# First queries repeated by PE with 0/1 matrices, keys projected ahead of queries, identity turns at the start, and scatters of rows moved, in a relative-attention and mixture-of-experts kernel

## The chip, the cores and the metric

The kernel runs on one core of one Trainium2 chip. The metric is device time in microseconds (us), the median of several executions; lower is better. The engines are PE (matmuls; its weight loads are shown apart as PEld), DVE, ACT and POOL, and SP, which here issues transfers. ACT and POOL issue some transfers too.

## The reference

`x` has 16 batches of 512 tokens with 128 features. The first half is attention with 16 heads of 8 features and relative positions, the second a mixture of 16 experts with one chosen for each token, and each has a layernorm (LN) ahead of it and one behind it.

```python
q, k, v = proj(Wq, bq), proj(Wk, bk), proj(Wv, bv)          # x normalized first
idx = jnp.clip(r[None, :] - r[:, None], -M, M) + M           # M = 128
rpk, rpv = rel_k[idx], rel_v[idx]
scores = (einsum('bhqd,bhkd->bhqk', q, k) + einsum('bhqd,qkd->bhqk', q, rpk)) / sqrt(hd)
w = softmax(scores)
out = einsum('bhqk,bhkd->bhqd', w, v) + einsum('bhqk,qkd->bhqd', w, rpv)
x = x + layernorm(out @ Wo.T + bo)
x = x + layernorm(moe(layernorm(x)))                         # top 1 of 16 experts, and a shared one
```

## The kernel before

All is in fp32. The attention loop (line 787) has 16 iterations for a batch, 256 in all, and a short tail. Iteration i belongs to batch b = i // 16, to c = (i % 16) // 4 and n = i % 4; k is i % 16. An iteration takes 32 queries (rows n * 128 + c * 32 on) of all 16 heads, as four tiles of 128 rows (32 queries times four heads) and 512 keys.

One iteration makes, in this order: the scores of its own queries (`scores`, line 377): four matmuls of the keys `km` with the expanded queries `qb`, and 32 small ones of the relative keys `relk` with the expanded queries `qr`; the turns (transposes by PE, `turn`, line 420) of the weights of iteration i - 1; DVE's negated maximum `nmax` and ACT's exponential for its own four tiles; the attention of iteration i - 5 (`attend`, line 473): 32 matmuls `pa<-wT,v`, and 48 short ones `pa<-wT,relv` for the near relative values (`attend_near`, line 509); and one more job for the single bank of `ps_o`, called `spare`. Score tiles have five banks of PSUM (`ps_s`), turns two (`ps_t`).

`qb` repeats the queries of 16 groups of eight with a 0/1 mask of heads, `qr` repeats them over positions with the mask `mq`. For `qr` the queries stand in another order on the partitions (`qz`): ACT writes `qp` (line 268), SP copies it to DRAM (`qd`, line 273), and 16 small transfers bring it back as `qz` (`queries_turned`, line 280). `expand` (line 357) then makes `qb` and `qr` on POOL, for the four iterations of one c, three iterations ahead (line 876).

The batch's own work is spread over the loop: statistics of the next x (k = 0 and 2), LN's root on POOL (`rstd_of`, line 75, a power), normalization, the turn of x (k = 6), queries (7), keys (14), values (15). `keys_mixed` and `keys_advance` keep, on POOL, the four copies of the keys `km` with the end values of the relative keys added.

For batch 0 the same work stands ahead of the loop (lines 768 to 785): statistics, LN with DVE, turn of x, queries, keys, `qz` (half of the transfers on ACT's queue), values, `expand(0, 0)`, `keys_mixed`, the load of x of batch 1 and `later_loads` (line 172).

`route` (line 602) takes a batch's attention output through both LNs, the router's logits and the counting of rows per expert, in 16 steps; it is a generator, and the loop takes one step at each of the listed places (line 865). Its last four steps are `pool.indirect_dma_start` (line 761): POOL scatters 128 rows of `pay` to `rows` in DRAM. Route r starts in k = 6 of batch r + 1; its scatters stand at the ends of k = 6, 7, 9 and 10 of batch r + 2, behind that iteration's key advance on POOL's queue. In k = 0, 4, 8 and 12 stands `sums` (line 428): DVE's reciprocal `rt` and POOL's copy `rb`, which PE turns, ACT copies to `R`, and POOL multiplies to `Rh` and `Rz`.

The order on PE, ACT, DVE, POOL and SP in the attention part is the order of the program text (`InOrder`, line 39); engines wait for each other by semaphores. After the loop, 73 blocks of 128 rows go through their experts (from line 881); between iterations 10 and 30 SP clears `rows` in 20 pieces (line 809).

```python
        for f in (x_turn, queries, keys):
            f(0)()
        queries_turned(0)
        values(0)()
        expand(0, 0)
```

Of the kernel before, what the change touches and what calls it, by code (L numbers as in the profile page):

```python
# [17 lines left out]
P = 128  # L18
# [3 lines left out]
HD = 8  # L22
# [28 lines left out]
def relative_attention_then_moe(  # L51
# [42 lines left out]
    with ExitStack() as actx:  # L94
# [11 lines left out]
        def load_x(b):  # L106
            x_sb[b] = bp.tile([P, NKT, D], F32, tag="x", name=f"x_sb{b}", bufs=4)

            for n in range(NKT):
                sp_q.dma_start(  # L110
                    x_sb[b][n * 32 : (n + 1) * 32], x[b, n * P : (n + 1) * P].rearrange("(c q) d -> q c d", q=32)
                )

        load_x(0)


        wq = wp.tile([P, D], F32, name="wq")
        wk = wp.tile([P, D], F32, name="wk")
# [14 lines left out]
        LR = 511  # L133
        rext = wp.tile([HD, LR], F32, name="rext")
        act.dma_start(bq_c, bq.rearrange("(p o) -> p o", o=1))
        act.dma_start(wq, WqT)
        act.dma_start(rext[:, 127 : 127 + NR], rel_kT)
        act.dma_start(wk, WkT)
        act.dma_start(bk_c, bk.rearrange("(p o) -> p o", o=1))
        act.dma_start(wv, WvT)  # L140
        act.dma_start(bv_r.rearrange("p h d -> p (h d)"), bv.partition_broadcast(P))
# [2 lines left out]
        for i in range(2):  # L144
            sp_q.dma_start(
                kend[:, i : i + 1], bass.AP(rel_kT.tensor, rel_kT.offset + i * (NR - 1), [[0, H], [NR, HD], [1, 1]])
            )
        act.mul(bq_c, bq_c, qscale)
        bk_hi = wp.tile([P, 1], F32, name="bk_hi")
        relk = wp.tile([P, 504], F32, name="relk")  # L150
# [69 lines left out]
        def bank(shape, name):  # L220
            return ps_o.tile(shape, F32, tag="o", name=name)
# [6 lines left out]
        def x_norm(b, eng=pool, between=None):  # L228

            mv = batch[b]["mv"]  # L230
            rs = rstd_of(sp, mv, NC, "lx", dve, pool)
            if between is not None:
                between()
            xn = bp.tile([P, NC, D], F32, tag="xn", name=f"xn{b}", bufs=1)
            for c in range(NC):
                eng.tensor_scalar(
                    xn[:, c, :], x_sb[b][:, c, :], mv[:, c, 0:1], rs[:, c : c + 1],
                    ALU.subtract, ALU.mult,
                )
            batch[b]["xn"] = xn  # L240
# [13 lines left out]
        def queries(b):  # L254


            xT = batch[b]["xT"]
            pq = bank([P, S], f"pq{b}")
            pe.matmul(
                pq.rearrange("p (c n q) -> p c n q", n=NKT, c=NC), wq,  # L260
                xT.rearrange("p (n c q) -> p c n q", n=NKT, c=NC), start=True, stop=True,
            )
            qp = bp.tile([P, TQ, S // TQ], F32, tag="qp", name=f"qp{b}")
            qz = bp.tile([P, 8, S // TQ], F32, tag="qz", name=f"qz{b}")
            batch[b].update(qp=qp, qz=qz)

            def leave():
                act.activation(
                    qp.rearrange("p q t -> p t q"), pq.rearrange("p (t q) -> p t q", q=TQ),
                    AF.Identity, bias=bq_c, scale=qscale,  # L270
                )
                qd = dp.tile([P, TQ, S // TQ], F32, tag="qd", name=f"qd{b}", bufs=2)
                sp_q.dma_start(qd, qp)
                batch[b]["qd"] = qd
                if b > 0:
                    queries_turned(b)

            return leave

        def queries_turned(b):  # L280
            qz, qd = batch[b]["qz"], batch[b]["qd"]
            for e in range(2):
                for i in range(TQ):
                    r = e * 64 + (7 - i) * HD
                    queue = act if b == 0 and i % 2 else sp_q
                    queue.dma_start(
                        qz[r : r + HD], qd[e * 64 : (e + 1) * 64, i, :].rearrange("(h d) t -> d h t", d=HD)
                    )

        def keys(b):  # L290

            pk = bank([P, S], f"pk{b}")
            pe.matmul(pk, wk, batch[b]["xT"], start=True, stop=True)
            kT = bp.tile([P, S], F32, tag="kT", name=f"kT{b}")
            batch[b]["kT"] = kT
            batch[b]["km"] = {}

            def leave():
                if b == 0:

                    km, hi = mixed(b, 0)
                    act.activation(km[:, 0:hi], pk[:, 0:hi], AF.Identity, bias=bk_c)
                    act.activation(km[:, hi:S], pk[:, hi:S], AF.Identity, bias=bk_hi)
                act.activation(kT, pk, AF.Identity, bias=bk_c)

            return leave

# [29 lines left out]
        def values(b):  # L337

            xT = batch[b]["xT"]
            pv = bank([P, NKT, D], f"pv{b}")  # L340
            for t in range(NKT):
                pe.matmul(pv[:, t, :], xT[:, t * P : (t + 1) * P], wv, start=True, stop=True)
            v = bp.tile([P, 3, NKT, D], F32, tag="v", name=f"v{b}")
            batch[b]["v"] = v

            def leave():
                if b == 0:
                    for t, n in ((v_lo, 0), (v_hi, 1)):
                        dve.tensor_copy(t, vend[:, n : n + 1, :].to_broadcast([P, H, HD]))
                row = lambda t, n: t.rearrange("p h d -> p (h d)").unsqueeze(1).to_broadcast([P, n, D])  # L350
                dve.tensor_add(v[:, 0], pv, row(bv_r, NKT))
                pool.tensor_add(v[:, 1, 0:2], v[:, 0, 0:2], row(v_lo, 2))
                pool.tensor_add(v[:, 2, 2:4], v[:, 0, 2:4], row(v_hi, 2))

            return leave

        def expand(b, c):

            bt = batch[b]
            tt = slice(c * 16, (c + 1) * 16)  # L360
            qb = up.tile([P, 16, HH, TQ], F32, tag="qb", name=f"qb{b}_{c}")
            pool.tensor_mul(
                qb,
                bt["qp"][:, :, tt].rearrange("p q t -> p t q").unsqueeze(2).to_broadcast([P, 16, HH, TQ]),
                mh4.unsqueeze(1).unsqueeze(3).to_broadcast([P, 16, HH, TQ]),
            )
            qr = up.tile([P, 16, 8, TQ], F32, tag="qr", name=f"qr{b}_{c}")
            pool.tensor_mul(
                qr,
                bt["qz"][:, :, tt].rearrange("p h t -> p t h").unsqueeze(3).to_broadcast([P, 16, 8, TQ]),  # L370
                mq.unsqueeze(1).unsqueeze(1).to_broadcast([P, 16, 8, TQ]),
            )
            batch[b, c] = (qb, qr)

        ORDER = (0, 2, 1, 3)

# [51 lines left out]
        def sums(b, c):  # L428

            rt = sp.tile([P, NKT, HG], F32, tag="rt", name=f"rt{b}_{c}")  # L430
            dve.reciprocal(rt, wts[b, c][1])
            rb = up.tile([P, NKT, HG, 32], F32, tag="rb", name=f"rb{b}_{c}", bufs=1)
            pool.tensor_copy(rb, rt.unsqueeze(3).to_broadcast([P, NKT, HG, 32]))
            batch[b, c, "rb"] = rb
# [333 lines left out]
        for c in range(NC):  # L768
            x_stats(0, c)
        x_norm(0, dve, relative_keys)  # L770
        dve.tensor_reduce(mh4, mh.rearrange("p (g h) -> p h g", h=HH), AX.X, ALU.add)
        dve.tensor_add(mq, mi[:, 0, :], mi[:, 1, :])
        dve.tensor_reduce(mz, mz4.rearrange("p g q -> p q g"), AX.X, ALU.add)
        dve.tensor_reduce(msum, mj.rearrange("p j g d -> p g d j"), AX.X, ALU.add)
        dve.tensor_add(bk_hi, bk_c, kend[:, 1:2])
        for f in (x_turn, queries, keys):
            f(0)()
        queries_turned(0)
        values(0)()
        expand(0, 0)  # L780
        for n in range(1, NKT):
            keys_mixed(0, n)
        if B > 1:
            load_x(1)
        later_loads()
        routes = {}
        for i in range(total + 24):
# [15 lines left out]
                routes[b - 1, 1] = route(b - 1, NC - 1, NC)  # L803
            if n == 0 and 0 <= i - 4 < total:
                sums(*at(i - 4)[:2])
                spare = lambda: sums_turn(*at(i - 4)[:2])
            if n == 1 and i >= 9 and i - 9 < total:
                spare = lambda: output(*at(i - 9)[:2])
            if 10 <= i < 30:
                clear_rows((i - 10) * NBLK // 20, (i - 9) * NBLK // 20)  # L810
            if nxt is not None:
# [48 lines left out]
            for r in sorted(routes):  # L860

                if r[0] < B - 2:
                    turns = i - (r[0] + 1) * 16 - 6 in (0, 1, 2, 3, 4, 5, 6, 7, 12, 13, 14, 15, 16, 17, 19, 20, 21)
                else:
                    turns = {7: 2, 9: 0, 12: 0, 13: 2, 15: 2}.get(k, 1) if live else 1
                for _ in range(turns):
                    bank_user = next(routes[r], StopIteration)
                    if bank_user is StopIteration:  # L870
                        del routes[r]
                        break
                    elif bank_user is not None:
                        bank_user()()
# [198 lines left out]
```

## Time and profile before

| what | value |
|---|---|
| median of 3 timed runs | 1917.79 us (1917.73 to 1917.93) |
| profiled execution, its own time | 1931.33 us |
| its span, first to last instruction | 1929.6 us |
| mean granted TensorE clock | 0.988 |
| busy share: PE, PEld, DVE, ACT, POOL | 97%, 72%, 79%, 63%, 51% |
| start of the first `nmax` (iteration 0) | 26.39 us |
| start of the last iteration's `nmax` | 1652.34 us |
| length of batches 2 to 14, `nmax` to `nmax` | 101.9 to 102.5 us |

The profile is of one execution with the recording on, which is why its time lies above the median. A row of a timeline has the start, the time, the engine, the line, the operation, the tiles written and read, the number of merged instructions, and in brackets the idle time of the engine just before with what ended it. Line 47 is the helper that keeps the order, so most rows carry L47 and are told apart by their tiles; buffer numbers are left out of names. "issue" means that the engine waited for nothing that the profile shows. The starts of the four `nmax` of an iteration give each iteration's length; in batches 2 to 14 iterations of the same k agree within some hundredths of a microsecond.

### The profile page before, as it was taken

How to read it: one execution, taken by the hardware profiler on the slowest of the kernel's cores; microseconds unless marked ns; L12 is line 12 of the kernel's file. 1: busy time of each engine (PE TensorE's matmuls, PEld its weight loads, DVE VectorE, ACT ScalarE, POOL GpSimd, SP SyncE). 2: the span in 40 equal slices, each digit the busy share in tenths (PEclk: the TensorE clock that was granted, in tenths of full speed). 3: DMA queues.
4: the chain of work that ended last, by engine and by line, in shares of the span. 5: the costliest groups of instructions: out<-in, count | busy, mean ns of one | idle time of the engine just before them, and what ended most of it. 6: DMA issues, size and time to landing. Idle time of an engine off the chain costs nothing. (4 is left out here: it accounts for less than half of the span.)

```text
span 1929.6 us, 88255 instructions
## 1 busy us (share of the span) xinstructions
PE 1863.7 (97%) x38268; PEld 1383.0 (72%) x38268; DVE 1528.7 (79%) x4009; ACT 1207.7 (63%) x3077; POOL 989.8 (51%) x1389
## 2 busy tenths in 40 slices
PE   6999999999999999999999999999999999779997
PEld 3667776776777777676767676776767776579997
DVE  4777787878788878788888888787878787757776
ACT  3666666666666666666666666666666665257775
POOL 4345455546455554546454555454645545236666
PEclk9999999999999999999999999999999999879999
DMA  2321100000000000000000000000000000066662
GB/s 77 65 35 40 17 23 5 15 14 5 24 5 24 4 24 3 25 3 25 3 24 5 24 4 16 12 13 16 5 18 5 18 3 9 9 176 180 183 182 87
DMA packets 88328, 68.64 MB, mean 36 GB/s; under 512 B 26440, under 2 KB 74341, under 8 KB 87809
## 3 DMA queue, kind: packets, MB, share of 16 engines
q1 hardware_dynamic: 81248, 53.60, 10.3%
q0 software_dynamic: 4384, 8.57, 1.4%
q8 instruction: 301, 4.93, 1.0%
q10 hardware_dynamic: 2304, 0.80, 0.2%
q14 instruction: 91, 0.74, 0.1%
HBM read 44.79 MB, written 18.75 MB: 33 GB/s over the span
## 5 line engine op out<-in xcount | busy, mean ns | idle before, releaser
L47 ACT ACTIVATE w<-ps,nmax 128x512 f32<-128x512 f32 x1024 | 699.0, 693 | 554.4 <-DVE nmax L47 554.0
L47 DVE TENSOR_REDUCE nmax<-ps 128x1 f32<-128x512 f32 x1024 | 655.1, 681 | 226.4 <-PE ps L47 225.2
L47 PE MATMUL pt<-ident,w 128*128 128x128 f32 x4096 | 562.0, 280 | 4.4 <-DVE wT L47 3.8
L47 PEld LDWEIGHTS pt<-ident,w 128*128 128x128 f32 x4096 | 439.7, 141 | 125.6 <-issue 85.7
L47 DVE COPY wT<-pt 128x512 f32<-128x512 f32 x512 | 348.3, 680 | 1.1 <-PE pt L47 0.7
L47 ACT COPY wT<-pt 128x512 f32<-128x512 f32 x512 | 300.9, 588 | 28.5 <-PE pt L47 26.5
L47 PE MATMUL ps<-km,qb 32*128 32x512 f32 x2048 | 298.4, 647 | 3.5 <-POOL qb L47 3.5
L47 PEld LDWEIGHTS ps<-relk,qr 64*32 64x32 f32 x8192 | 124.4, 106 | 227.6 <-issue 183.9
L47 PE MATMUL pa<-wT,v 128*32 128x128 f32 x8192 | 276.7, 276 | 2.5 <-DVE oz L47 1.4
L47 PE MATMUL ps<-relk,qr 64*32 64x288 f32 (+4 forms) x8192 | 275.5, 378 | 0.0
L47 PEld LDWEIGHTS pa<-wT,v 128*32 128x32 f32 x8192 | 208.1, 109 | 45.2 <-issue 36.0
L47 ACT ACTIVATION_READ_ACCUMULATOR w<-ps,nmax 128x1 f32 x1024 | 211.8, 207 | 0.0
L47 PE MATMUL pa<-wT,relv 128*32 128x48 f32 (+1 forms) x12288 | 199.3, 211 | 6.2 <-issue 5.4
L47 POOL TENSOR_TENSOR Rh<-R,mh 128x512 f32<-128x512 f32 x64 | 66.6, 1040 | 261.0 <-ACT R L47 253.8
L47 PEld LDWEIGHTS pa<-wT,relv 128*32 128x32 f32 x12288 | 186.8, 110 | 11.1 <-issue 11.1
L47 POOL TENSOR_TENSOR qr<-qz,mq 128x1024 f32<-128x1024 f32 x64 | 137.3, 2146 | 0.0
L47 PEld LDWEIGHTS ps<-km,qb 32*128 32x128 f32 x2048 | 82.4, 184 | 59.9 <-issue 32.0
L47 POOL TENSOR_SCALAR km<-kT,kend 128x32 f32<-128x32 f32 (+2 forms) x223 | 115.6, 520 | 1.7 <-PE ps L47 0.9
L47 POOL COPY km<-kT 128x32 f32<-128x32 f32 (+3 forms) x207 | 53.0, 261 | 113.8 <-ACT kT L47 113.8
L47 POOL DMA_INDIRECT out_dram<-f,to x73 | 75.9, 1039 | 46.8 <-issue 26.9
L47 DVE TENSOR_TENSOR od<-pa,Rh 128x128 f32<-128x128 f32 x256 | 72.9, 285 | 32.6 <-PE pa L47 29.7
L47 POOL COPY rb<-rt 128x512 f32<-128x512 f32 x64 | 39.2, 612 | 112.3 <-DVE rt L47 112.1
(168 smaller groups left out, 2331.0 us busy)
## 6 DMA issues: line engine op xcount, KB each, us to landing
gu<-_L_ffn_gate_up_proj_dram SPq DMA_DIRECT2D x73, 256.0 KB
dn<-in_L_ffn_down_proj_dram SPq DMA_DIRECT2D x73, 128.0 KB
rows<-zero SPq DMA_DIRECT2D x19, 266.0 KB
xc<-rows SPq DMA_DIRECT2D x8, 532.0 KB
x_sb<-in_L_attn_x_dram SPq DMA_DIRECT2D x64, 64.0 KB
qd<-qp SPq DMA_DIRECT2D x16, 256.0 KB
qz<-qd SPq DMA_DIRECT2D x248, 16.0 KB
relv<-vext SPq DMA_DIRECT2D x1, 1536.0 KB
```

What stands on the lines that cost most here:

```text
L47: return lambda *a, **k: self.tc.keep_in_program_order(op(*a, **k))
```

## The change

Five things are changed, all in the attention part.

1. `warm(52)`: PE makes 52 turns of the identity into a tile that nobody reads, as its first work.
2. Loads: `wk` goes ahead of `wq` on ACT's queue; x of batch 1 is loaded on SP right behind `kend`, ahead of `kext`, and not after the preparation of batch 0.
3. The preparation of batch 0: keys are projected ahead of queries, into a bank of `ps_s`. ACT writes the first `km`, then only the first 16 of 64 columns of `qp`, then `kT`, then the other 48. PE repeats the first 16 columns with eight 0/1 matrices `sel` (128x128 each), which POOL makes behind LN's root by one memset and eight selects, in a buffer of tag `wT`; DVE makes the first `qb`, and the first `qr` from PE's banks. Only the other 48 columns go through DRAM to `qz`, with all 16 transfers on SP.
4. The values of batch 0 become the `spare` job of iteration 2.
5. Routes 0 to 12 take their last four steps, the scatters, in the iterations with n = 0, right behind `sums` (so behind `rb` and ahead of `Rh` on POOL): k = 8 and 12 of batch r + 2, and k = 0 and 4 of batch r + 3. Routes 13 to 15 stay as they were.

```diff
+        def warm(n):
+            idle = ps_t.tile([P, NKT, P], F32, tag="t", name="idle")
+            for t in range(n):
+                pe.transpose(idle[:, t % NKT, :], ident, ident)
+        warm(52)
...
+        act.dma_start(wk, WkT)
         act.dma_start(wq, WqT)
         act.dma_start(rext[:, 127 : 127 + NR], rel_kT)
-        act.dma_start(wk, WkT)
...
+        if B > 1:
+            load_x(1)
         act.mul(bq_c, bq_c, qscale)
...
+        def repeat_queries(rep_q):
+            for h in range(8):
+                pe.matmul(
+                    rep_q[h // 4][:, h % 4].rearrange("p t q -> p q t"), sel[:, h * P : (h + 1) * P],
+                    batch[0]["qp"][:, :, 0:16], start=True, stop=True,
+                )
+        def expand_first(rep_q):
...
+            dve.tensor_mul(
+                qb,
+                batch[0]["qp"][:, :, 0:16].rearrange("p q t -> p t q").unsqueeze(2).to_broadcast([P, 16, HH, TQ]),
+                mh4.unsqueeze(1).unsqueeze(3).to_broadcast([P, 16, HH, TQ]),
             )
+            for i in range(2):
+                dve.tensor_mul(
+                    qr[:, :, i * 4 : (i + 1) * 4, :].rearrange("p t h q -> p h t q"), rep_q[i],
+                    mq.unsqueeze(1).unsqueeze(1).to_broadcast([P, 4, 16, TQ]),
+                )
...
+        sel = up.tile([P, 8 * P], F32, tag="wT", name="sel")
+        nc.gpsimd.memset(sel, 0.0)
+        for h in range(8):
+            nc.gpsimd.affine_select(
...
-        for f in (x_turn, queries, keys):
-            f(0)()
-        queries_turned(0)
-        values(0)()
-        expand(0, 0)
+        x_turn(0)()
+        leave_k = keys(0)
+        leave_q = queries(0)
+        rep_q = [ps_t.tile([P, 4, 16, TQ], F32, tag="t", name=f"rep_q{i}") for i in range(2)]
+        leave_k()
+        leave_q(0, 16)
+        repeat_queries(rep_q)
+        leave_k(False)
+        expand_first(rep_q)
+        leave_q(16, S // TQ)()
         for n in range(1, NKT):
             keys_mixed(0, n)
-        if B > 1:
-            load_x(1)
         later_loads()
...
                 sums(*at(i - 4)[:2])
+                for r in sorted(routes):
+                    if r[0] < B - 3 and i - (r[0] + 1) * 16 - 6 >= 18:
+                        if next(routes[r], StopIteration) is StopIteration:
+                            del routes[r]
...
+            if i == 2:
+                spare = lambda: values(0)
...
-                if r[0] < B - 2:
+                if r[0] < B - 3:
+                    turns = i - (r[0] + 1) * 16 - 6 in (0, 1, 2, 3, 4, 5, 6, 7, 12, 13, 14, 15)
+                elif r[0] < B - 2:
                     turns = i - (r[0] + 1) * 16 - 6 in (0, 1, 2, 3, 4, 5, 6, 7, 12, 13, 14, 15, 16, 17, 19, 20, 21)
```

More of the change, by code (lines that the diff above doesn't have):

```diff
@@ L265, in queries, with leave, turned @@
             batch[b].update(qp=qp, qz=qz)
-            def leave():
+            qd = dp.tile([P, TQ, S // TQ], F32, tag="qd", name=f"qd{b}", bufs=2)
+            def leave(t0=0, t1=S // TQ):
                 act.activation(
-                    qp.rearrange("p q t -> p t q"), pq.rearrange("p (t q) -> p t q", q=TQ),
+                    qp[:, :, t0:t1].rearrange("p q t -> p t q"),
+                    pq[:, t0 * TQ : t1 * TQ].rearrange("p (t q) -> p t q", q=TQ),
                     AF.Identity, bias=bq_c, scale=qscale,
                 )
-                qd = dp.tile([P, TQ, S // TQ], F32, tag="qd", name=f"qd{b}", bufs=2)
-                sp_q.dma_start(qd, qp)
-                batch[b]["qd"] = qd
+                if b == 0 and t0 == 0:
+                    return
+                sp_q.dma_start(qd[:, :, t0:t1], qp[:, :, t0:t1])
+                def turned():
+                    for e in range(2):
+                        for i in range(TQ):
+                            r = e * 64 + (7 - i) * HD
+                            sp_q.dma_start(
+                                qz[r : r + HD, :, t0:t1],
+                                qd[e * 64 : (e + 1) * 64, i, t0:t1].rearrange("(h d) t -> d h t", d=HD),
+                            )
                 if b > 0:
-                    queries_turned(b)
-            return leave
[L280 to L288, printed above, removed]
+                    turned()
+                return turned
+            return leave
         def keys(b):
-            pk = bank([P, S], f"pk{b}")
+            pk = bank([P, S], f"pk{b}") if b > 0 else ps_s.tile([P, S], F32, tag="s", name="pk0")
             pe.matmul(pk, wk, batch[b]["xT"], start=True, stop=True)
@@ L296, in keys, with leave @@
             batch[b]["km"] = {}
-            def leave():
-                if b == 0:
+            def leave(first=b == 0):
+                if first:
                     km, hi = mixed(b, 0)
@@ L303, in leave @@
                     act.activation(km[:, hi:S], pk[:, hi:S], AF.Identity, bias=bk_hi)
-                act.activation(kT, pk, AF.Identity, bias=bk_c)
+                else:
+                    act.activation(kT, pk, AF.Identity, bias=bk_c)
             return leave
@@ L355, in values, with expand @@
             return leave
-        def expand(b, c):
+        def expand(b, c, eng=pool, parts=((0, 16),)):
             bt = batch[b]
-            tt = slice(c * 16, (c + 1) * 16)
             qb = up.tile([P, 16, HH, TQ], F32, tag="qb", name=f"qb{b}_{c}")
-            pool.tensor_mul(
+            qr = up.tile([P, 16, 8, TQ], F32, tag="qr", name=f"qr{b}_{c}")
+            batch[b, c] = (qb, qr)
+            for t0, t1 in parts:
+                n, tt = t1 - t0, slice(c * 16 + t0, c * 16 + t1)
+                eng.tensor_mul(
+                    qb[:, t0:t1],
+                    bt["qp"][:, :, tt].rearrange("p q t -> p t q").unsqueeze(2).to_broadcast([P, n, HH, TQ]),
+                    mh4.unsqueeze(1).unsqueeze(3).to_broadcast([P, n, HH, TQ]),
+                )
+                eng.tensor_mul(
+                    qr[:, t0:t1],
+                    bt["qz"][:, :, tt].rearrange("p h t -> p t h").unsqueeze(3).to_broadcast([P, n, 8, TQ]),
+                    mq.unsqueeze(1).unsqueeze(1).to_broadcast([P, n, 8, TQ]),
+                )
@@ new lines, in repeat_queries @@
+        def repeat_queries(rep_q):
[3 more added lines that the diff above has]
+                    batch[0]["qp"][:, :, 0:16], start=True, stop=True,
+                )
+        def expand_first(rep_q):
+            qb = up.tile([P, 16, HH, TQ], F32, tag="qb", name="qb0_0")
+            qr = up.tile([P, 16, 8, TQ], F32, tag="qr", name="qr0_0")
+            batch[0, 0] = (qb, qr)
+            dve.tensor_mul(
@@ L363, in expand @@
                 qb,
-                bt["qp"][:, :, tt].rearrange("p q t -> p t q").unsqueeze(2).to_broadcast([P, 16, HH, TQ]),
+                batch[0]["qp"][:, :, 0:16].rearrange("p q t -> p t q").unsqueeze(2).to_broadcast([P, 16, HH, TQ]),
                 mh4.unsqueeze(1).unsqueeze(3).to_broadcast([P, 16, HH, TQ]),
             )
[L367 to L372, printed above, removed]
@@ L373, in expand @@
-            batch[b, c] = (qb, qr)
+            for i in range(2):
+                dve.tensor_mul(
+                    qr[:, :, i * 4 : (i + 1) * 4, :].rearrange("p t h q -> p h t q"), rep_q[i],
+                    mq.unsqueeze(1).unsqueeze(1).to_broadcast([P, 4, 16, TQ]),
+                )
         ORDER = (0, 2, 1, 3)
@@ L770, in relative_attention_then_moe @@
         x_norm(0, dve, relative_keys)
+        sel = up.tile([P, 8 * P], F32, tag="wT", name="sel")
+        nc.gpsimd.memset(sel, 0.0)
+        for h in range(8):
+            nc.gpsimd.affine_select(
+                sel[:, h * P : (h + 1) * P].rearrange("p (e j d) -> p e j d", e=2, j=TQ),
+                sel[:, h * P : (h + 1) * P].rearrange("p (e j d) -> p e j d", e=2, j=TQ),
+                [[-64, 2], [0, TQ], [-1, HD]], ALU.not_equal, 1.0, base=-h * HD, channel_multiplier=1,
+            )
         dve.tensor_reduce(mh4, mh.rearrange("p (g h) -> p h g", h=HH), AX.X, ALU.add)
```

## The prediction

> **What bounds the kernel now.** I read the page's slices first, then the timeline of the first 50 us, then the start of every iteration: a block of 32 queries takes four iterations, a batch 16 (k = 0 to 15), and each opens with the DVE maximum `nmax`.
>
> ```profile
> PE   6999999999999999999999999999999999779997
> ```
>
> PE is full everywhere but in the first slice and in the experts near the end, which the change doesn't touch. So there are two places to gain: the first slice, where PE waits, and the loop, where only a pause of PE itself counts. The timeline of the first slice (start us, duration us, engine, line, operation, tiles, count, idle time before it and what ended it):
>
> ```profile
> 9.04 1.24 PE L47 MATMUL ptx<-ident,xn 128*128 128x128 f32 x4 [9.04 <-DVE xn L47]
> ...
> 10.96 2.07 PE L47 MATMUL pq<-xT,wq 128*128 128x512 f32 x2 [0.68 <-ACT xT L47]
> ...
> 17.83 2.07 PE L47 MATMUL pv<-wv,xT 128*128 128x128 f32 x8 [1.51 <-ACT kT L47]
> ...
> 22.07 1.32 POOL L47 TENSOR_TENSOR qb<-qp,mh 128x512 f32<-128x512 f32 x1
> 23.34 2.12 POOL L47 TENSOR_TENSOR qr<-qz,mq 128x1024 f32<-128x1024 f32 x1
> ...
> 23.44 2.09 PE L47 MATMUL ps<-km,qb 32*128 32x512 f32 x8 [3.54 <-POOL qb L47]
> ...
> 25.52 1.32 PE L47 MATMUL ps<-relk,qr 64*32 64x160 f32 x32
> ...
> 26.39 2.48 DVE L47 TENSOR_REDUCE nmax<-ps 128x1 f32<-128x512 f32 x4 [5.77 <-PE ps L47]
> ...
> 33.39 3.40 PE L47 MATMUL pt<-ident,w 128*128 128x128 f32 x16
> ...
> 36.72 1.14 PE L47 MATMUL ps<-km,qb 32*128 32x512 f32 x8
> ```
>
> It is one chain: LN, turn, queries, keys, values, POOL's two values additions, POOL's qb and qr, scores. The queries' round trip through DRAM (qd issued 14.22, the last qz 19.43) ends beside it. PE is slow until about 36 us: the same eight score passes take 2.09 at 23.44 and 1.14 at 36.72; a 128x512 projection takes 2.07 here and 1.04 in batch 5. The granted clock reads 1.00 in this stretch, but the trace's first clock record starts at 36.18, full speed, where a turn's pitch falls from 0.213 to 0.109 us. So I go by durations.
>
> In the loop, I compare batch 1 (no scatter falls in it) with batch 5, for k = 9, PE's timeline:
>
> ```profile
> 185.31 0.75 PE L47 MATMUL pa<-wT,relv 128*32 128x64 f32 x48
> ```
>
> ```profile
> 592.85 0.29 PE L47 MATMUL pa<-wT,relv 128*32 128x64 f32 x7
> 593.38 0.71 PE L47 MATMUL pa<-wT,relv 128*32 128x64 f32 x41 [0.24 <-issue]
> ```
>
> and POOL's in batch 5:
>
> ```profile
> 592.04 1.07 POOL L47 DMA_INDIRECT rows<-pay,at_i  x1 [0.16 <-issue]
> ```
>
> The 48 near-value matmuls take 0.75 us; with a scatter begun 0.81 before them, PE stops issuing for some 0.45 and they last 1.24. Iteration 9 is 7.03 us in batch 1 and 7.45 to 7.62 in batches 2 to 14 (7.50 typical); iteration 11, with its scatter 0.83 ahead of those matmuls, is 5.94 and 6.23. The other two scatters, run in iterations 5 and 7, cost nothing: their pause falls on turns or score matmuls (6.65 against 6.74; 6.42 against 6.42).
>
> **The change, part by part.**
>
> *Identity turns.* 52 turns need only `ident` (POOL, done at 1.65); PE's sequencer was waiting by 0.80. At the slow pitch of 0.213 us the block would take 11.1 us. The trace bears on whether turns bring the clock up: full speed came at 36.18 after turns had filled most of the time since 33.39, while matmuls from 26.77 to 33.4 had not brought it. If one to two times 3.41 us of turns do it (my estimate: turns ran for 2.8 before 36.18, and the one spell at half clock in the loop, from 97.62, lasts 3.41), 16 to 32 run slow and the rest at 0.109: the block ends between 9.0 and 10.7 us. x's four normalized pieces are ready from 8.9 to 9.76, so it costs 0 to 1. I take 0. The Trainium skill, "TensorE: Matmul & The Clock Gate", Part 4, says against this that a transpose does not count as PE-busy in the same way and does not bring the full clock; by it, the block would end at 12.8. The turns of 33.39 to 36.18 speak against the rule here.
>
> *Chain to the first scores, at full speed.* The last xn is ready at 9.76 as before; its turn 0.27, to 10.08. xT on ACT 0.58 and two handovers: keys start at 10.75. Projections 1.1 each: keys to 11.85, queries to 12.8. ACT's two km pieces (0.29 pitch, 0.55) run beside the queries. The first 16 of 64 query columns: 1.12 for 64, a small ACT operation takes 0.20, so about 0.43; to 13.3. Eight repeats with `sel`, two passes each: eight passes of pv took 1.13 in the loop, so 2.2; to 15.5. DVE's qb (0.65 estimated from the 0.69 of the equal-sized v addition) is over by 14.0; the qr halves, 0.69 each, by 16.25. Key scores 1.14 to 16.6, relative scores 0.67 (192 columns took 0.72): nmax at **17.2** instead of 26.39, **-9.2**.
>
> What must be ready: `sel` on POOL behind the root (done 8.62): a memset of 1024 columns about 0.9 (0.20 for 128, 0.11 for 16), eight selects at the 0.37 pitch of mj's: to 12.7, 0.6 ahead of need. If DVE's xn slows POOL, up to 1 us late. relk's packets end by 13; x's next four loads are issued on SP ahead of kext (1.74 of issue, from 5.2 to 7.0, and kext waits until 7.72 for DVE's copies), so only their bytes can delay it: 3.5 us of cover. km of iteration 1 on POOL: kT at 14.0 plus 1.2, needed at 17.3. wq moves behind wk: needed at 11.85, issued by 1.8.
>
> *First iterations.* Iteration 0 to 1 was 6.19: the fourth key score waits for the third exponential, 2.9 after nmax, then 1.07 and 0.88 at full speed: 4.85, **-1.3**. Iteration 1 to 2 had slow turns, 6.08; at the pace of the next, 5.25 with a few more columns: **-0.8**. Values move into iteration 2, where PE goes straight from turns to scores: **+1.1** (1.13 on PE; DVE's 0.69 and POOL's 1.45 lie beside it, and attention needs them only in iteration 5). All 16 qz copies now go on SP: 16 x 0.41, from 17 to 24, landed by 26; qr of the second block on POOL is then ready at 28, needed at 35. Queued behind that wait on POOL are key advances for iteration 5 on, the values' additions and the next LN's root, all due after 40. The other new waits hold back nothing else: PE's repeats wait 0.5 for ACT's first queries, DVE's qr halves for the repeats, and behind both stand only the scores that need them. Behind them SP's relv is late by some 1.5, at 33, needed at 44. Sum of the start: **-10.2** (bounds -8 to -11).
>
> *Scatters.* For routes 0 to 12 the four scatters go from iterations 5, 7, 9, 11 (as they run) to behind `rb` in k = 8, 12, and 0, 4 of the next batch. In POOL's queue they stand ahead of Rh, which waits for ACT's R for another 4 us anyway. Gone: 0.47 + 0.29 = 0.76 a batch. New: I place each start at rb's end plus 0.16 and compare with the near-value matmuls. k = 8 and 12: 2.3 us and more ahead (in iteration 5 a scatter 2.3 ahead cost nothing). k = 0: after them, over score matmuls as in iteration 7. k = 4 (batch 5): rb ends 559.69, scatter 559.85, matmuls at 560.73, 0.88 ahead, next to the costly 0.81 and 0.83; one scatter of batch 15, 1.25 ahead, cost 0.02. Bounds 0 and 0.49; I take 0.3, by the nearer row. 13 x (0.76 - 0.3) = **-6.0** (bounds -3.5 to -9.9).
>
> *Unknown.* In batch 0's iteration 11 PE stops once for 1.94 ("issue") amid the clearing of `rows`, and then runs slow for a while: 9.11 against 5.94. About 140 added PE instructions shift what is fetched when: bounds -3.2 and +3.2, I take 0.
>
> Sum: -16.2. The profiled execution took 1931.33 (span 1929.6) and would take 1915.1; the median of the timed runs, 1917.79, is 0.7% under it, and less 16.2 it is **1901.6**.
>
> **Rivals.**
> - *The scatters buy nothing*: their pause only moves, or is a product of the recording (profiled runs are 13.5 longer). For it: k = 4's distance; against it: two of four old places cost nothing. 1917.8 - 10.2 = 1907.6.
> - *Turns don't bring the clock up.* The block then ends at 12.8, x_turn at 13.9, keys and queries 2.07 each, repeats 3.8: nmax at 25.85, -0.5; values +1.1; scatters -6.0: 1912.4. Against it: 36.18. This is what the page cited above would give.
> - *The repeated queries arrive, but something else holds the first scores* (sel, relk, km): all of the start's gain goes only if it is 9 us late, and the covers above are 0.6 to 3.5: 1911.8.
> - *Slower: the scatter's pause hits PE at all four new places.* If PE's turns and score matmuls there starve as the near-value matmuls do, each costs 0.47: 13 x (1.88 - 0.76) = +14.6, less 10.2: 1922.2. It decides where a new place costs over 0.39 on average (13 x (4c - 0.76) = 10.2). Against it: iterations 5 and 7.
>
> **Chances.** Forecast 0.65, scatters nothing 0.19, slow turns 0.07, other hold 0.04, slower 0.05. 0.2% (3.8 us, to 1913.9) is about what a measurement of this kernel can tell. The two near 1912 lie close to it; half of them counts as same: faster 0.89, same 0.06, slower 0.05. The range takes in the first two cases with their bounds: from 1917.8 - 11 - 9.9 and part of the unknown, 1895, to 1917.8 - 9 with no gain by scatters, 1909.
>
> **What would show it.** Turn pitch falling to 0.11 before 9 us and pq at 1.1; repeats beginning at 13.3 and nmax at 17.2; iterations 0 to 3 of 4.9, 5.3 and 6.3; iteration 9 at 7.03 and 11 at 5.94 in batches 2 to 14, iteration 4 longer by about 0.3. I am wrong if pq is still 2.07, if PE waits for `sel`, or if k = 4, 8, 12 or 0 grows by as much as 9 and 11 shrink.

## The result, and the profile after

| | kernel before | kernel after |
|---|---|---|
| median of 5 timed runs | 1917.79 us (1917.53 to 1918.56) | 1908.89 us (1908.00 to 1910.67) |
| ratio | | 0.9954 (95% interval 0.9944 to 0.9965) |
| profiled execution, own time and span | 1931.33, 1929.6 | 1909.82, 1908.0 |

The change gains 8.9 us, where 16.2 was forecast: the time lies in the range given, but 7.3 us above the number. One thing stands out at once: the profiled execution of the kernel before was 13.5 us longer than its timed runs, that of the kernel after only 0.9.

The slices of the kernel after say that PE is full as before, but for the same slices of the experts near the end; the first has gone from 6 to 8 tenths.

```profile
PE   8999999999999999999999999999999999679997
```

The timeline of its first 30 us, cut to the chain (start us, duration us, engine, line, operation, tiles, count, and in brackets the idle time before with what ended it):

```profile
1.71 7.86 PE L47 MATMUL idle<-ident 128*128 128x128 f32 x52 [1.71 <-POOL ident masks.py:199]
...
8.52 0.94 POOL L812 MEMSET sel<- 128x1024 f32 x1
8.59 1.80 DVE L47 TENSOR_SCALAR xn<-x_sb,mvx,lx_rs 128x128 f32<-128x128 f32 x4 [0.95 <-POOL lx_rs L47]
9.53 2.90 POOL L814 TENSOR_SCALAR_AFFINE_SELECT sel<-sel 128x128 f32<-128x128 f32 x8
...
11.45 1.13 PE L47 MATMUL pk<-xT,wk 128*128 128x512 f32 x2 [0.67 <-ACT xT L47]
...
12.41 1.02 PE L47 MATMUL pq<-xT,wq 128*128 128x512 f32 x2
...
14.04 1.09 DVE L47 TENSOR_TENSOR qb<-qp,mh 128x512 f32<-128x512 f32 x1 [3.00 <-ACT qp L47]
...
14.15 2.02 PE L47 MATMUL rep_q<-qp,sel 128*128 128x128 f32 x16 [0.72 <-ACT qp L47]
...
16.10 1.14 PE L47 MATMUL ps<-km,qb 32*128 32x512 f32 x8
...
16.21 0.69 DVE L47 TENSOR_TENSOR qr<-rep_q,mq 128x512 f32<-128x512 f32 x1 [0.20 <-PE rep_q L47]
...
17.76 2.49 DVE L47 TENSOR_REDUCE nmax<-ps 128x1 f32<-128x512 f32 x4 [0.86 <-PE ps L47]
```

This is the chain that was forecast. The projections take 1.13 and 1.02, not 2.07, so PE runs at full speed; the repeats take 2.02 at 14.15; the first `nmax` starts at 17.76 and not at 26.39. DVE's second `qr` half is over at 16.90, inside the key scores, so PE goes on without a wait. One thing on the chain is slower than forecast: the four `xn` take 1.80 (1.12 before), while POOL makes `sel` beside them. `qb` is slower too, 1.09 where 0.65 was taken, but it is over at 15.13, and DVE still waits for the repeats.

The prediction's test of the scatters was iteration 9 at 7.03 and 11 at 5.94. They read 7.04 and 5.94, and iteration 4 reads 6.08, unchanged. That looks like the whole of the 9.9 us, and more than forecast. But the time does not show it, and that is what the experiments are about.

### The profile page after: what moved, and what is told of

It is laid out like the page before. It is cut to its first block, busy times and chain, and to the rows that moved or that the text cites. A ratio compares the mean times of both kernels' runs of the same rounds, so it can differ in the third digit from the quotient of the medians.

```text
span 1908.0 us, 88414 instructions
## 1 busy us (share of the span) xinstructions
PE 1856.4 (97%) x38336; PEld 1385.4 (73%) x38336; DVE 1530.5 (80%) x4012; ACT 1208.3 (63%) x3078; POOL 990.6 (52%) x1396
## 3 DMA queue, kind: packets, MB, share of 16 engines
q1 hardware_dynamic: 82720, 53.60, 10.6%
## 5 line engine op out<-in xcount | busy, mean ns | idle before, releaser
L47 PE MATMUL pa<-wT,relv 128*32 128x48 f32 (+1 forms) x12288 | 191.8, 211 | 0.0
L47 DVE TENSOR_REDUCE oT<-od 128x32 f32<-128x128 f32 x256 | 94.8, 370 | 0.0
```

The source lines that it names most:

```text
L47: return lambda *a, **k: self.tc.keep_in_program_order(op(*a, **k))
```

## The experiments

The three main theories that the expectations name: **A**, PE's pause behind a scatter is there in every execution, and moving the scatters takes it away; **B**, the pause comes with some executions (in the first expectations) or with the recording (in the later ones), and the timed, unrecorded runs have few or none; **C**, the pause is there on some chips and not on others. "Kernel before, beside it" is its median on the same chip at the same time. The runs fell on four chips, numbered 8, 2, 3 and 11, each used at one time only.

### The two halves alone (chip 8)

*e1_before_again*: the kernel before, unchanged.

> The kernel before, unchanged, for a second profile. The first profiled execution took 1931.33 us where the timed runs take 1917.8, and it held 13 pauses of 0.47 and 13 of 0.29 us (9.9 us) at near-value matmuls behind scatters, and one of 3.2 us amid the clearing of rows: 13.1 us together, nearly the whole difference of 13.5. Theory A: the pauses belong to the kernel, in every run; then this profile shows iteration 9 at 7.50 and iteration 11 at 6.23 again. Theory B: the pauses come and go with the execution, and the timed runs have few of them; then this profile may show 7.03 and 5.94, and its own time lies near 1918 if it does.

Measured: 1931.48 recorded, and 1932.58 (1928.35 to 1936.30, 11 runs) unrecorded; iteration 9 7.50, iteration 11 6.23. So the pause is not a product of the recording: on this chip the kernel before takes 1932 without it too.

*e2_start_only*: the kernel after with the scatters back at the ends of k = 6, 7, 9 and 10.

```diff
-                for r in sorted(routes):
-                    if r[0] < B - 3 and i - (r[0] + 1) * 16 - 6 >= 18:
...
-                if r[0] < B - 3:
-                    turns = i - (r[0] + 1) * 16 - 6 in (0, 1, 2, 3, 4, 5, 6, 7, 12, 13, 14, 15)
-                elif r[0] < B - 2:
+                if r[0] < B - 2:
```

> The changed kernel with the scatters put back at the ends of k = 6, 7, 9 and 10. Theory A (pauses in every run, so the scatters brought 9.9 us): about 1917.8 to 1918.8, as the start then brought nothing in timed runs. Theory B (timed runs have no such pauses): about 1908.9, the whole of the change is the start: the first nmax at 17.8 instead of 26.4, and the first three iterations 1.0 shorter in sum.

Measured: 1923.92, ratio 0.9956 (0.9943 to 0.9969), -8.7. The first `nmax` at 17.74; iterations 9 and 11 still 7.53 and 6.23.

*e3_scatters_only*: the kernel before with only the scatters moved, the reverse of that diff.

> The kernel before with only the scatters of routes 0 to 12 moved behind rb. Theory A: 13 x 0.76 = 9.9 us faster, about 1907.9. Theory B: no change, 1917 to 1918.5. Its profile shows iteration 9 at 7.03 and 11 at 5.94 by both, and its profiled execution lies within 3 us of its timed runs by B.

Measured: 1924.13, ratio 0.9957 (0.9944 to 0.9969), -8.5. Iterations 9 and 11 fall to 7.04 and 5.94; iteration 4 grows from 6.08 to 6.15 and iteration 5 from 6.65 to 6.74. Its PE and POOL timelines in iteration 4 of batch 5:

```profile
557.89 1.06 PE L47 MATMUL pa<-wT,relv 128*32 128x64 f32 x48
```

```profile
557.00 1.12 POOL L47 DMA_INDIRECT rows<-pay,at_i  x1 [0.17 <-issue]
```

The 48 near-value matmuls, 0.89 behind the scatter, take 1.06 and not 0.75: the pause does fall on them at the new place, as the prediction feared, but half of it is made up before the next `nmax`; the two iterations together lose 0.16, not 0.3. On this chip the start is worth a little less than was forecast (8.7 of 10.2) and the scatters more (8.5 where 6.0 was forecast), each within its bounds.

### The kernel after without its turns (chip 8)

*e4_no_turns*:

```diff
-        warm(52)
```

> The changed kernel without the 52 identity turns. My theory: they bring PE to full speed; without them the turn of x starts at 9.0 and not 9.6, but keys and queries take 2.07 each, the repeats 3.8 and the first key scores 2.07: first nmax at about 22.4 instead of 17.8, the next two iterations 1.4 and 0.8 longer: 1908.9 + 6.8 = about 1915.7. Rival (turns of the identity do nothing for the speed, which some other part of the new start brings): the same speeds as with them, and the start 0.6 us earlier: 1908.3.

Its PE timeline:

```profile
11.66 2.07 PE L47 MATMUL pk<-xT,wk 128*128 128x512 f32 x2 [0.68 <-ACT xT L47]
13.53 1.75 PE L47 MATMUL pq<-xT,wq 128*128 128x512 f32 x2
15.99 2.02 PE L47 MATMUL rep_q<-qp,sel 128*128 128x128 f32 x16 [0.72 <-ACT qp L47]
```

Measured: 1917.65 (1912.03 to 1919.82), ratio 0.9920 (0.9905 to 0.9934), -14.9; first `nmax` at 19.61, and 22.4 was expected. The keys' projection runs slow, but the queries' is already getting faster, the clock's first record at full speed starts at 14.98, and the repeats take 2.02 as with the turns. So the turns are worth 1.85 us of the chain to the first `nmax`; PE's own work from 9.7 to 15 brings the clock up without them. Even the 1.85 is not always kept: iteration 3 starts at 36.16 here, and with the turns at 34.31 and 34.35 (the kernel after, e8), but at 35.28 and 36.54 in e2 and e5, where the clock falls again in between. In the total, 1.85 is less than the interval's half width of 2.8.

### The whole again, and the scatters at the worst place (chip 2)

*e6_before_third* (the kernel before) and *e5_after_again* (the kernel after), both unchanged:

> The kernel before, for its profile on this chip. Theory C: if its time is near 1918, iterations 9 and 11 of batches 2 to 14 are near 7.03 and 5.94 and not 7.50 and 6.23; if it is near 1932, they are 7.50 and 6.23.

> The changed kernel again. The kernel before took 1917.8 us beside it in the first timing and 1932.6 on the chip of the first experiments, where the start alone brought 8.7 and the scatters alone 8.5. Theory C: PE's pauses behind scatters belong to the chip; where the kernel before takes about 1932, this takes 1932.6 - 17 = about 1915, and where it takes about 1918, this takes about 1909. Theory D: the two parts don't add, since both end in the same wait: about 1923 where before takes 1932.

Measured: the kernel before 1931.91 recorded and 1931.54 beside it unrecorded, iteration 9 7.49, iteration 11 6.20; the kernel after 1916.59 (1913.81 to 1917.34), ratio 0.9921 (0.9907 to 0.9935), **-15.0**. The same two kernels whose ratio was 0.9954 in the result are 0.9921 here, and the intervals don't overlap. What differs is the kernel before, 13.8 us longer; the kernel after is 7.7 longer. Of that, 2.2 is seen in its first three iterations (4.75, 5.31 and 6.49 in the result's profile; 5.95, 6.31 and 6.49 here); batches 2 to 14 are 1.5 longer, where the pause falls in iterations 4 and 5, batch 15 is 1.2 longer, and what comes behind the last `nmax` 2.5. The stretches around the fall of the clock, with PE's busy time, granted clock, DMA share and GB/s:

```profile
18.00:20.97 2.97, 2.64 (x7) 1.00 0.02 6
20.97:27.80 6.83, 6.83 (x50) 0.50 0.15 29
```

PE fell back to half the clock for 6.83 us; in e2_start_only for 3.41 (from 22.02).

*e7_scatters_only_again*: e3's kernel.

> The kernel before with only the scatters moved, again. Theory C: 8.5 to 10 us faster than before on a chip where before takes about 1932, within 1.5 us of it where before takes about 1918. Theory D: 8.5 to 10 faster on any chip.

Measured: 1922.90, ratio 0.9957 (0.9944 to 0.9971), -8.6, with iterations 4, 5, 9 and 11 as in e3 to 0.03. The parts alone, 8.7 on chip 8 and 8.6 here, make 17.3; together they measured 15.0, which by its interval is 12.6 to 18.0. So they add up within the noise, and Theory D of e5's expectation (about 1923) falls.

*e8_scatters_at_near_values*: the kernel after, with its scatters at the ends of k = 9, 10, 13 and 1, meant to start about 0.8 ahead of near-value matmuls.

```diff
-                for r in sorted(routes):
-                    if r[0] < B - 3 and i - (r[0] + 1) * 16 - 6 >= 18:
...
-                    turns = i - (r[0] + 1) * 16 - 6 in (0, 1, 2, 3, 4, 5, 6, 7, 12, 13, 14, 15)
+                    turns = i - (r[0] + 1) * 16 - 6 in (0, 1, 2, 3, 4, 5, 6, 7, 12, 13, 14, 15, 19, 20, 23, 27)
```

> The changed kernel with the four scatters of routes 0 to 12 at the ends of k = 9, 10, 13 and of k = 1 of the next batch, so that each begins about 0.8 us ahead of near-value matmuls. Theory C, on a chip like the second (before about 1932): pauses of 0.47, 0.29, 0.47 and 0.47 a batch, 13 x 1.7 = 22 us over the changed kernel. On a chip like the first (before about 1918): within 3 us of the changed kernel. Rival (the place of a scatter counts by what it delays on POOL, not by PE's pause): the same few us on both.

Measured: 1938.34 (1936.04 to 1939.65), ratio 1.0037 (1.0023 to 1.0051), 21.7 over e5. Iteration 1 is 7.71 (6.74), 9 is 7.49, 11 is 6.19, 13 is 6.91 (6.67). PE's and POOL's timelines in iteration 1 of batch 5:

```profile
536.64 0.92 PE L47 MATMUL pa<-wT,relv 128*32 128x64 f32 x36
538.01 0.38 PE L47 MATMUL pa<-wT,relv 128*32 128x48 f32 x12 [0.46 <-issue]
```

```profile
536.71 1.07 POOL L47 DMA_INDIRECT rows<-pay,at_i  x1 [0.15 <-issue]
```

PE goes on for 0.84 after the scatter has started, more slowly (36 matmuls in 0.92, where 48 take 0.75 elsewhere), then stops for 0.46, with nothing in the trace that it waits for. Here the scatter starts 0.07 behind the first matmul, not 0.8 ahead, and the stop has moved with it. The expectation's 22 us come out in the sum, in unrecorded runs, but not by its parts: iterations 9, 11, 13 and 1 lose 0.46, 0.25, 0.24 and 0.97 where 0.47, 0.29, 0.47 and 0.47 were expected. So on this chip the pause is real, and the place of the scatter decides whether it costs time; the distance alone does not give its size (0.82 in iteration 9 and 0.83 to 0.85 in iteration 11 cost 0.46 and 0.25).

### A reworked start, and the turns alone (chip 3)

*e9_reworked*: the kernel after with `sel` made ahead of LN's root, POOL's constants for the routes and the zeroes behind `keys_mixed`, 46 turns, the values of batch 0 in iteration 0, and no scatter in k = 4.

```diff
-        warm(52)
+        warm(46)
...
-                    if r[0] < B - 3 and i - (r[0] + 1) * 16 - 6 >= 18:
+                    for _ in range({18: 1, 22: 1, 26: 3}.get(i - (r[0] + 1) * 16 - 6, 0) if r[0] < B - 3 else 0):
...
-            if i == 2:
+            if i == 0:
                 spare = lambda: values(0)
```

> The changed kernel with four edits that the profiles point to: the 0/1 matrices made ahead of LN's root and POOL's other constants behind the first mixed keys, so that POOL doesn't slow DVE's normalization (1.80 us for four in the changed kernel, 1.12 before); 46 identity turns; the values of batch 0 as the spare job of iteration 0, where PE waits for banks, and not of iteration 2; the scatter of k = 4 moved to stand behind that of k = 0. Against the changed kernel: first nmax at 17.0 instead of 17.8, iteration 2 at 5.3 to 5.4 instead of 6.5, and on a chip with pauses k = 4 and 5 shorter by 0.17 in sum in 13 batches (2.2): 4.0 us in all, so about 19 under before where before takes about 1932 and about 11 under it where before takes about 1918. Rival (iteration 0 has no room for the values, or the two scatters in a row in k = 0 pause PE): nothing gained on the changed kernel, 15 and 9 under before.

Measured: 1909.43 (1907.60 to 1911.09), with 1919.31 beside it for the kernel before: ratio 0.9952 (0.9938 to 0.9966), -9.9. DVE's timeline:

```profile
8.60 1.12 DVE L47 TENSOR_SCALAR xn<-x_sb,mvx,lx_rs 128x128 f32<-128x128 f32 x4 [0.95 <-POOL lx_rs L47]
...
17.09 1.29 DVE L47 TENSOR_REDUCE nmax<-ps 128x1 f32<-128x512 f32 x2 [0.87 <-PE ps L47]
```

With POOL idle beside them the four `xn` take 1.12 again, and the first `nmax` starts 0.67 earlier; iterations 0 to 2 take 15.32 instead of 16.54. But 1.77 of these 1.9 us are lost in iterations 11 to 13 (22.24 against 20.47), where PE stops for 1.88 ("issue") amid the clearing of `rows` (0.92 in the kernel after). So its ratio cannot be told from that of the kernel after.

*e10_turns_only*: the kernel before with `warm(52)` and nothing else.

```diff
+        warm(52)
```

> The kernel before with the 52 identity turns and nothing else of the change. If turns bring the clock up, queries, keys and values take 1.1 each and not 2.07, but keys still wait for ACT's 1.12 for the queries and POOL's qb and qr still follow the values and the round trip: relative scores at about 23.2 instead of 25.5, then PE slow again after its wait of 3.5 us: 2.4 us faster than before. Rival (by the rule that transposes don't count, the block is slow and ends at 12.8): 3 us slower than before.

```profile
11.25 1.12 PE L47 MATMUL pq<-xT,wq 128*128 128x512 f32 x2 [0.68 <-ACT xT L47]
13.59 1.94 PE L47 MATMUL pk<-xT,wk 128*128 128x512 f32 x2 [1.21 <-ACT qp L47]
17.03 2.07 PE L47 MATMUL pv<-wv,xT 128*128 128x128 f32 x8 [1.51 <-ACT kT L47]
```

Measured: 1916.32, ratio 0.9986 (0.9977 to 0.9995), -3.0, with the first `nmax` at 25.61. The turns bring the full clock, it is lost again at 13.8, behind PE's wait of 1.21 (the records show half until 34.2), and about 0.8 us is left at the first `nmax`; the rest of the 3.0 is within the interval, which begins at -1.0.

The other reading of this run was a surprise: its scatters stand at the old places, and iterations 9 and 11 are 7.04 and 5.94. This chip has no pause. That speaks for Theory C, and one more pair of runs tested it.

### The scatters alone, on a chip without the pause (chip 11)

*e12_before_fourth* is the kernel before, *e11_scatters_only_third* e3's kernel.

> The kernel before unchanged, for its iterations on the same chip. Theory C: where it takes about 1918 unrecorded, its profile has iteration 9 at 7.04 and iteration 11 at 5.94 in batches 2 to 14 and the profiled run too takes about 1919; where it takes about 1932, 7.50 and 6.22. Theory B: 7.50 and 6.22 in every profile, whatever the unrecorded time. Theory A: 7.50 and 6.22, with 1932 unrecorded.

> The kernel before with only the scatters moved, once more, since the gain of this part should hang on the chip. Theory C (PE's pause behind a scatter belongs to some chips): if the kernel before takes about 1918 beside it, there is no pause to take away, so the time is within 2 us of it (ratio 0.999 to 1.001) and batches take 101.2 to 101.4; if the kernel before takes about 1932 beside it, the ratio is 0.9957 as in the two earlier runs. Theory A (the pause comes with the old places on every chip): 0.9955 either way. Theory B (the pause comes with the recording): 1.000 either way.

Measured: the kernel before 1920.38 recorded, 1920.87 (1917.57 to 1923.22, 15 runs) unrecorded, iterations 9 and 11 at 7.04 and 5.94. With the scatters moved 1919.56, ratio **0.9993** (0.9984 to 1.0002), the same two iterations at 7.04 and 5.94: nothing gained. PE's and POOL's timelines of the kernel before in iteration 9 of batch 5, the place that the prediction shows:

```profile
590.60 0.75 PE L47 MATMUL pa<-wT,relv 128*32 128x64 f32 x48
```

```profile
589.79 1.07 POOL L47 DMA_INDIRECT rows<-pay,at_i  x1 [0.16 <-issue]
```

The scatter starts 0.81 ahead of the matmuls, to the hundredth as in the prediction's lines, and they take 0.75 in one piece. The idle time of PE ahead of all 12288 near-value matmuls (us, times), first in the profile of before that the prediction was made from, then here:

```profile
  issue: 5.4, 16
```

```profile
  issue: 3.1, 2
```

Both of these stops, 2.76 and 0.30, lie in iterations 11 and 12 of batch 0, where there are no scatters. Theory C stands: same program, same order, same distances, and the pause is there in every profile from chips 8 and 2 (four each) and in none from 3 and 11. A and B both fall, A by this pair, B by e1, e6 and e8. One thing is left untested: as no chip was used at two times, the pause may belong to the time of the runs, or to what else went on there, and not to the chip itself.

## Why the prediction was right or wrong

The stretches of the span show where the time went. Each is from one `nmax` to another (us); the middle column is e12's profile, in which PE doesn't pause.

| stretch | before, as in the prediction | before, no pause | after |
|---|---|---|---|
| to the first `nmax` | 26.39 | 26.58 | 17.76 |
| iterations 0 to 2 | 17.53 | 16.68 | 16.54 |
| 3 to 10 | 47.94 | 47.95 | 48.23 |
| 11 to 13 | 22.20 | 22.12 | 20.47 |
| 14, 15 and batch 1 | 113.48 | 114.25 | 113.50 |
| batches 2 to 14 | 1326.91 | 1317.12 | 1316.28 |
| batch 15, to its last `nmax` | 97.89 | 97.79 | 96.75 |
| the rest | 277.28 | 276.10 | 278.48 |
| span | 1929.63 | 1918.58 | 1908.01 |

**The step that failed is the scatters' -6.0.** The pause itself was read rightly from the profiled execution: there batches 2 to 14 took 9.8 us longer than in the middle column, close to 13 times the 0.76 of the prediction. What was wrong is the step from that execution to the median, "less 16.2 it is 1901.6". The 13.5 us between the two were taken for the recording, as the section on the profile says, and the recording costs nothing: e12 took 1920.38 with it and 1920.87 without. The profiled execution came from a place with the pause, and the timed runs, at 1917.79, lie 1.5 and 3.1 under the medians of chips 3 and 11, which have none, and 13.8 and 14.8 under those of chips 2 and 8. So the pause that the scatters were to take away was not in the median. This is argued from the times; the record names no chip for the result's runs, and there is no profile of the kernel before that goes with the timed runs. But the kernel after has one that belongs to its own: its scatter of iteration 4 starts 0.88 ahead of the near-value matmuls, and they run through in 0.75, in batch 5 as in the others, where on chips 8 and 2 they take 1.01 to 1.07 at that distance.

```profile
547.21 0.75 PE L47 MATMUL pa<-wT,relv 128*32 128x64 f32 x48
```

```profile
546.33 1.12 POOL L47 DMA_INDIRECT rows<-pay,at_i  x1 [0.17 <-issue]
```

So the rival "the scatters buy nothing", at 1907.6, is what happened, by a way that it did not name: the pause neither moved nor came from the recording; it was not there. That the time still lies in the range is luck as far as the scatters go: the range took in this rival, to which 0.19 was given, and the measurement is 0.1 under its upper end of 1909, which stands for no gain by the scatters. The prediction's own test, iterations 9 and 11 at 7.03 and 5.94, could not tell the two cases apart, since a run without the pause reads the same. On a chip that has the pause the forecast's sum nearly holds: -15.0 against -16.2.

**The other terms, by their own runs:**

- *Turns bring the clock up*: right. In the kernel after the first record at full clock starts at 5.78, and two windows of its timeline give 0.22 us a turn ahead of it (19 turns in 4.26) and 0.12 behind it (35 in 4.18). The Trainium skill, "TensorE: Matmul & The Clock Gate", Part 4, has it that transposes do not bring the full clock; here turns of the identity in fp32 did, with nothing else on PE, in all six profiles with 52 or 46 of them (after, e2, e5, e8, e9, e10; first full clock at 4.96 to 7.32). But the price of their absence was mis-sized: of the rival's +8.65 at `nmax`, 3.8 came from the slow block itself and 4.8 from a PE that stays slow for the whole chain, and e4, which has no block, measured +1.85.
- *Chain to the first scores*, -9.2: measured -8.6. The difference is the four `xn`, 0.68 more: keys start at 11.45 and not 10.75, and what stands behind them stays 0.6 to 0.9 late (0.56 at `nmax`). The prediction asked only whether `xn` slows POOL; here DVE slowed, and in e9, where `sel` is made earlier, it did not. `sel`, done at 12.43, `relk` and `km` held nothing.
- *First iterations*, -1.3 and -0.8: 6.19 to 4.75 and 6.08 to 5.31 in the two profiles, as forecast. But these are not constants: without the pause the kernel before has 5.52 and 5.90, and the kernel after had 5.95 and 6.31 on chip 2. They hang on when the clock falls, and that differs between executions (at 20.97 in e5, at 22.02 in e2, in the kernel after not before 1644). Against the middle column these two iterations gain 1.4 and not 2.1, and all three, with the values, only 0.1.
- *Values into iteration 2*, +1.1: 5.25 to 6.49, +1.24. e9 has it back (5.26) with the values in iteration 0.
- *The stop in batch 0* (the prediction's "Unknown"), 0 with bounds of 3.2: -1.7 in this profile. It wanders: 19.9 to 23.1 for iterations 11 to 13 over all runs, and from 20.4 to 23.0 in three executions of one kernel (e3, e7, e11). The rest behind the last iteration's `nmax`, which the sum does not name, wanders more: 276.0 to 281.0 over all runs, and 276.0 to 280.0 in the same three.
- *k = 4*, 0.3 a batch: 0.16 on chip 8, 0.11 to 0.13 on chip 2, nothing where there is no pause.

The start alone was forecast at -10.2 and brought 8.7 on chip 8; if the scatters brought nothing in the result, it is the whole 8.9 there. Both are within its bounds of -8 to -11.

**What stays open**: why PE pauses on some chips and not on others, and what stops it there (no view shows a releaser). For the other stops the traces give a hint. Their DMA queue q8, of kind "instruction", brings a packet of 16 KB every 5.7 us (median). Between 45 and 1600 us PE stops 24 times in all profiles for over 0.1 with "issue" and no scatter just before, and 23 of these stops, the long ones of batch 0 among them, end 1.3 to 1.8 after the end of such a packet. Ahead of the 17 stops of over 0.7 that packet came 6.6 to 10.6 after the one before. For the 79 stops behind scatters that distance is anything from 0.0 to 6.3. So the stops of batch 0 go with late packets of instructions, and the pause behind a scatter does not. Whether the clearing of `rows` is what makes them late is not shown, since no version without it was run.

## What to carry to other kernels

When a profiled execution is clearly longer than the timed runs, find out where the difference sits before any of it is sold as gain: a pause that is missing from the median can't be removed from it. Run the kernel before again, recorded and unrecorded on one chip, and compare iterations of one kind: two times that agree show that the recording is free, and two chips that disagree in one iteration name the place. The chain ahead of the loop was forecast here to 0.6 us from rows; it can be done if each engine's neighbours are asked about too, and if a clock that turns bring up is counted only for the work that would not have brought it up itself.

## What the runs showed of the hardware

- The same program takes 1918 to 1921 us on two chips and in the runs of the result, and 1932 on two others, at the same mean granted clock (0.989 in e12, 0.988 in the first profile). 9.8 of the 11 us between these two are a pause of PE behind an indirect transfer of POOL. Where it occurs, 48 near-value matmuls that start 0.8 to 1.0 after the transfer take 0.94 to 1.37 and not 0.75, and 1.75 where they start 0.07 ahead of it (e8). It costs nothing where the scatter falls over turns and score matmuls (iterations 5 and 7 of before).
- PE falls back to half the clock for 3.41 or 6.83 us in the first iterations (e2, e5), where it waits now and then for other engines. It costs 1.0 to 2.2 us and differs between executions of one kernel.
- On PE's "issue" stops away from scatters: 23 of 24 end 1.3 to 1.8 after a packet of the instruction queue q8 (all 14 profiles).
- DVE's four `xn` take 1.80 with POOL's memset and selects beside them and 1.12 without (e9).
